# A third pair of nodes in plain float32 in the last stage, the flag's loads tied to an output, and two node splits emitted earlier

## The chip, the cores and the metric

The kernel runs on one core of a Trainium2 chip. The metric is the device time of one execution in microseconds (us). Before the change three runs took 454.33, 454.55 and 456.33 us; their median is 454.55 us.

## What is computed

The reference is a small graph network on 2,500 nodes with 256 features and 80,000 edges sorted by their end node. Cut to what matters:

```python
h = max(layernorm(x), 0)
xs = [h]
for W, b in ((W0, b0), (W1, b1), (W2, b2)):      # three edge convolutions
    m = concat([h[dst], h[src] - h[dst]]) @ W + b
    h = relu(segment_sum(m, dst) / max(count, 1))
    xs.append(h)
return x + concat(xs) @ Wf + bf
```

## The kernel before, in words

The edge sums are done as matrix products. From the edge lists the kernel builds a matrix of edge counts (it lies in DRAM as `a_dram`, in bf16, in five groups of up to 512 columns), and a convolution is then a product of the counts with the node features, plus a product with the node's own features. That is `by_windows`. If some edge found no place in that scheme, a flag `missing` is set and `general` computes everything again behind a branch (`gnn_kernel`); for these inputs the flag stays 0.

**Layout.** 2,500 nodes are 20 tiles of 128, the last one not full, or Q = 10 pairs of tiles, q = 0 to 9; pair q holds tiles 2q and 2q + 1. `hT` holds the features of the present layer, transposed. `acc` holds the result, 20 tiles of 128 x 256, to which each layer's share of the last product is added (`add_to_acc`, on VectorE). At the end `acc` is written out.

**Products in three parts.** TensorE multiplies float32 quickly only in a reduced form (`fp32r`). So a float32 operand is first *split* (`Split`, line 1005): one ScalarE instruction makes the high part, two VectorE instructions (`rest`) make a low part and a mixed part. `times` (line 1234) then takes three products per chunk, twelve for a pair of tiles with 256 output columns. A pair in `PLAIN` (line 1484) is not split in the last stage: its product is taken from `hT` in plain float32, four matmuls in the program (lines 1571 to 1574), which stand in the profile as eight. Split parts lie in the pool `stage` (four buffers, tiles named `staged`, also used for the loads of counts) or, by `split_in_blocks` (line 1065), in the pool of `block` tiles.

**Order of the work.** Instructions of PE, DVE, ACT, POOL and SP that are issued through the wrapper `InOrder` (`PEo`, `DVEo` and so on) keep the order in which the program text emits them on their engine: an edge without a wait ties each to the one before. Anything else may be moved by the scheduler to where it takes the instruction's inputs to be ready. So the order in the text decides.

**Layers 1 and 2** (loop at line 1492). A *node stage* goes over the ten pairs in the order `orders[l]`. Step i multiplies pair `order[i]` (`Nodes.multiply`, which needs that pair's split), then `parts` takes the result from the banks (ScalarE scales it to `zf` and casts it to `zh`, VectorE makes `zl` and adds to `acc`; the last tile's `zf` is made on VectorE with `brow`), `combine` and `sums` make further forms, and `lone.multiply(i - 2)` does a part of the count product. At the end of step i the split of pair `order[i + 2]` is emitted (at i = 0 that of `order[3]`). A *stream stage* (`Stream`) then does the rest of the count products; its `tick` also emits the first splits of the next stage.

**The last stage** (line 1566) multiplies each pair of `orders[3]` by the last block of `Wf`: pair 8, 9, 0, 1 (split in the stream stage before), 2 (plain), 3 (split in blocks), 7 (plain), 6 (begun in the stream stage, its rest at i = 0), 5, 4. For each pair: products on PE, two `add_to_acc` on DVE, and the outputs. Up to i = 5 a pair (pair 9 excepted) goes out as one DMA of SP; from i = 6 on each tile goes alone, the first of a pair on SP's queue and the second on ACT's. Behind the adds of i = 1, 2, 3 stand the splits of pairs 3, 5 and 4.

**The flag** (line 1602). Each engine loads the flag into a register and branches on it (line 1607). SP's and POOL's loads run as soon as the flag is known. Those of PE, DVE and ACT are tied behind everything emitted on their engine. After the branch SP waits for the outputs, and all engines meet at the end of the program (line 1631).

Of the kernel before, what the change touches and what calls it, by code (L numbers as in the profile page):

```python
# [298 lines left out]
def by_windows(ctx: ExitStack, tc: tile.TileContext, x, src, dst, Ws, bs, Wf, bf, out, missing):  # L299
# [37 lines left out]
    Q = NT // 2  # L337
# [41 lines left out]
    def bank():  # L379
        return ps[-1].tile([P, 512], F32, name="bank")  # L380
# [75 lines left out]
    def load_wb(l, queue=SP):  # L456
        if l:
            new_raw(l)
        ws[l] = wpool.tile([P, DC, D], F32, name="wt"), raws[l][:, :, 0, :] if l else hot.tile([P, DC, D], F32, name="own_w0", bufs=1)
        queue.dma_start(ws[l][1], Ws[l][D:2 * D, :].rearrange("(c p) d -> p c d", p=P))  # L460

    def load_wt(l, queue=SP):
        queue.dma_start(ws[l][0], Ws[l][0:D, :].rearrange("(c p) d -> p c d", p=P))

    def load_wf(l, queue=SP):
        if l == L:
            new_raw(l)
        wfs[l] = raws[l][:, :, 1, :] if l else hot.tile([P, DC, D], F32, name="own_w1", bufs=1)
        queue.dma_start(wfs[l], Wf[l * D:(l + 1) * D, :].rearrange("(c p) d -> p c d", p=P))
# [24 lines left out]
    def load_b(l, queue=SP):  # L494
        queue.dma_start(brow[PAD:PAD + 1, :], bs[l].rearrange("(o d) -> o d", o=1))
# [39 lines left out]
    behind = pp.tile([P, WG * P], BF16, name="behind")  # L535
# [29 lines left out]
    ahead = []  # L565
# [258 lines left out]
    def group_of(g):  # L824
        return g * GS, min(GS, N - g * GS)
# [97 lines left out]
    order = """  # L923
# [73 lines left out]
    splits, coming = {}, []  # L997

    def block():
        return blocks[0].tile([P, 2, 512], F32R, name="block")  # L1000

    def flat(l):
        return raws[l].rearrange("p c t d -> p c (t d)") if l < L else wfs[l]
# [61 lines left out]
    def split_in_blocks(q, whole=True):  # L1065
        two = [block().rearrange("p c n -> p (c n)") for _ in range(2)]
        return Split(q, [two[0][:, :2 * D], two[0][:, 2 * D:], two[1][:, :2 * D]], whole)
# [356 lines left out]
    def all_found():  # L1424
        pf = bank()
        PEo.matmul(pf[0:1, 0:1], found, ones, start=True, stop=True)
        DVEo.tensor_scalar(missing, pf[0:1, 0:1], float(E), None, op0=OP.not_equal)
# [3 lines left out]
    def load_alone(k, order):  # L1431
        c = order[2 * k] // 2
        st = stage.tile([P, 8 * GS], BF16, name="staged").rearrange("p (t n) -> p t n", n=GS)[:, :4, :group_of(alone)[1]]
        SPo.dma_start(st, a_dram[alone][:, 4 * c:4 * c + 4, :group_of(alone)[1]])
        loaded[k] = st
# [45 lines left out]
                tick(n)  # L1481

    AHEAD_H = 2
    PLAIN = (2, 7)
    LAG = 2
    orders = [None, list(range(Q)), [8, 9, 0, 1, 2, 3, 7, 6, 5, 4], [8, 9, 0, 1, 2, 3, 7, 6, 5, 4]]
    def split(q):
        tile_ = stage.tile([P, 4 * GS], F32R, name="staged")
        Split(q, [tile_[:, k * 2 * D:(k + 1) * 2 * D] for k in range(3)])

    begun, bias = [], add_bf()
    for l in range(1, L):
        order = orders[l]
        lone = Alone(l, order)
        if l == 1:
            load_alone(0, order)
            split(order[2])
        pending = []
        stream = Stream(l)
        for i in range(Q + LAG):  # L1500
            if 0 < i <= Q:
                lone.make(i - 1)
            if i < Q:
                q = order[i]
                n = Nodes(l, q)
                n.multiply(splits.pop(q), coming[0])
                if i + AHEAD_H < Q and i % 2 == 1:
                    load_alone((i + 1) // 2, order)
                n.parts()
                n.combine()  # L1510
                ahead = i + AHEAD_H + (i == 0)
                if ahead < Q and order[ahead] not in splits:
                    split(order[ahead])
                pending.append(n)
            if i and pending:
                pending.pop(0).sums()
            if i == 1:
                for o in range(DC):
                    lone.own(o, 0)
                if l == 1:  # L1520
                    all_found()
            if i >= LAG:
                lone.multiply(i - LAG)
            if i == Q - 1:
                stream.load(3)
        room = stage.tile([P, 4 * GS], F32R, name="staged")
        stream.make(2)
        lone.end()
        turn_of[1] = 0
        if l + 1 < L:  # L1530
            load_b(l + 1, SPo)
            load_wb(l + 1, SPo)
            load_wt(l + 1, SPo)
        load_wf(l + 1, SPo)
        after = orders[l + 1]

        def tick(n):
            if (l, n) in AT["bias"]:
                next(bias)
            if n == AT["begun"] and l + 1 == L:  # L1540
                begun.append(split_in_blocks(6, False))
            if n == AT["wsum"]:
                combine(wsum, ws[l][0].rearrange("p c (o n) -> p (c o) n", o=2))
                own_forms.append(Forms(ws[l][0], [ws[l][0][:, c, :] for c in range(DC)],
                                       [room[:, k * DC * D:(k + 1) * DC * D].rearrange("p (c d) -> p c d", c=DC)
                                        for k in range(3)]))
            for k, step in enumerate(("high", "low", "across", "last")):
                if n == AT["forms"][k]:
                    getattr(own_forms[-1], step)()
            if n == AT["sub"] and l + 1 < L:  # L1550
                DVEo.tensor_sub(ws[l + 1][0], ws[l + 1][0], ws[l + 1][1])
            if n == AT["load"] and l + 1 < L:
                load_alone(0, after)
            for k in range(3 if l + 1 < L else 4):
                if n == AT["split"][k]:
                    split(after[k])
            for k, step in enumerate(("high", "low", "across", "last")):
                if n == AT["coming"][k]:
                    if k == 0:
                        raw = flat(l + 1)  # L1560
                        coming[:] = [Forms(raw, [raw[:, c, :] if l + 1 < L else raws[L][:, c, 0, :] for c in range(DC)])]
                    getattr(coming[0], step)()

        stream.run(tick)

    order = orders[L]
    for i, q in enumerate(order):
        po = bank()
        po = [po[:, :D], bank()[:, :D] if i == Q - 1 else po[:, D:]]
        for k in range(2):  # L1570
            if q in PLAIN:
                for c in range(DC):
                    PEo.matmul(po[k], hT[:, c, (2 * q + k) * P:(2 * q + k + 1) * P], wfs[L][:, c, :],
                               start=(c == 0), stop=(c == DC - 1))
            else:
                times(po[k], splits[q], k, coming[0])
        for k in range(2):
            t = 2 * q + k
            add_to_acc(t, po[k])
            n = P if t < NT - 1 else LAST  # L1580
            if i < Q - 4 and q < Q - 1:
                if k:
                    d = SPo.dma_start(out[(t - 1) * P:(t + 1) * P, :].rearrange("(k p) d -> p k d", p=P),
                                      acc[:, t - 1:t + 1, :])
            else:
                d = (ACTo if i >= Q - 4 and k else SPo).dma_start(out[t * P:t * P + n, :], acc[:n, t, :])
        if i == 0:
            begun[0].rest()
        elif i == 1:
            split_in_blocks(3)  # L1590
        elif i < 4:
            split((5, 4)[i - 2])


def gnn_kernel(tc: tile.TileContext, x, src, dst, Ws, bs, Wf, bf, out):
    nc = tc.nc
    with tc.tile_pool(name="flag", bufs=1) as flag:
        missing = flag.tile([1, 1], I32, name="missing")
        tc.mark_branch_hint_location("again", "LikelyTaken",
                                     engines=[getattr(mybir.EngineType, e) for e in ("PE", "DVE", "Activation")])  # L1600
        by_windows(tc, x, src, dst, Ws, bs, Wf, bf, out, missing)
        loads, (again,) = nc.values_load_multi_w_load_instructions(missing, min_val=0, max_val=1)

        for d in loads:
            if d.ins.engine in [getattr(mybir.EngineType, e) for e in ("PE", "DVE", "Activation")]:
                tc.keep_in_program_order(d)
        with tc.If(again > 0, label="again"):
            general(tc, x, src, dst, Ws, bs, Wf, bf, out)

# [27 lines left out]
```

## Time and profile before

| what | value |
|---|---|
| runs of before, us | 454.33, 454.55, 456.33 |
| the profiled execution's own time, us | 454.44 |
| its span, first to last instruction, us | 452.5 |
| mean granted clock of TensorE | 0.995 |
| ScalarE (ACT) busy, us | 326.2 (72%) |
| GpSimd (POOL) busy, us | 53.7 (12%) |
| HBM read, written | 35.23 MB, 18.14 MB |
| last stage's outputs | 1 x 68 KB, 5 x 128 KB and 5 x 256 KB on SP's queue, 4 x 128 KB on ACT's |

The profile comes from one execution. Its span leaves out what lies around the first and the last instruction, 1.94 us here. In a timeline row the first number is the start from the span's begin, the second how long the merged group took, then engine, line, operation, the tiles written and read, and the number of instructions; in brackets the idle time of the engine before it and what ended it. Nearly all instructions carry line 267, that of the `InOrder` wrapper, so they are told apart by their tiles: `bank<-block,staged` are products of split pairs, `bank<-wbf,hT` those of plain ones, `staged<-hT` the high part of a split (on ACT) or `staged<-hT,staged` its low part (on DVE). PEld is TensorE's weight load; one goes ahead of each matmul. A row of a table by stretches holds the stretch, its length, then busy time and number of instructions of the engines in the order PE, PEld, DVE, ACT, POOL (or of the one asked for), the granted clock, the mean busy share of the 16 DMA engines and GB/s.

### The profile page before, as it was taken

To read this page: it belongs to the slowest core of one execution; us is meant where nothing else is said; L and a number is where in the kernel's file an instruction comes from. 1 tells how busy PE (TensorE), PEld (TensorE's weight loads), DVE (VectorE), ACT (ScalarE), POOL (GpSimd) and SP (SyncE) were. 2 spreads that over 40 slices of the span, in tenths; PEclk is the share of its full clock that TensorE was granted. 3 is DMA by queue.
4 is the path that set the end of the run, shared out by engine and by line. 5 is a ranking of instruction groups with operands and counts; after the bars stand their busy time and mean duration, and the time that the engine had idled before them with its cause. 6 is when DMAs were issued, how large, how long until landed. Compare 5 with 4: busy or idle time off the path is not lost.

```text
span 452.5 us, 7520 instructions
## 1 busy us (share of the span) xinstructions
PE 441.5 (98%) x2755; PEld 360.1 (80%) x2755; DVE 379.4 (84%) x735; ACT 326.2 (72%) x610; POOL 53.7 (12%) x68
## 2 busy tenths in 40 slices
PE   7999999999999999999999999999999999999993
PEld 3888877888888889888878878867788788788793
DVE  7999999998899536399968958997999789589894
ACT  5898888777765427577789949875887898597630
POOL 4791201302006030100000000000000000000000
PEclk9999999999999999999999999999999999999998
DMA  8410199792959997611483432211135525241015
GB/s 275 118 39 1 24 198 165 88 170 35 202 117 109 183 245 124 136 43 44 167 314 92 151 131 95 93 42 41 42 83 183 211 94 185 94 124 62 1 65 167
DMA packets 34377, 53.77 MB, mean 119 GB/s; under 512 B 1963, under 2 KB 27774, under 8 KB 34334
## 3 DMA queue, kind: packets, MB, share of 16 engines
q0 software_dynamic: 14624, 19.00, 26.3%
q1 hardware_dynamic: 18206, 32.59, 22.3%
q10 hardware_dynamic: 1504, 1.63, 1.1%
q8 instruction: 23, 0.38, 0.3%
q14 instruction: 20, 0.16, 0.1%
HBM read 35.23 MB, written 18.14 MB: 118 GB/s over the span
## 4 chain that ended last, share of the span: by engine, by line


## 5 line engine op out<-in xcount | busy, mean ns | idle before, releaser
L267 ACT CAST block<-staged 128x1024 fp32r<-128x1024 bf16 (+1 forms) x120 | 116.8, 1026 | 1.7 <-DVE staged L267 1.6
L267 PE MATMUL bank<-a,zh 128*128 128x512 f32 (+1 forms) x200 | 79.5, 397 | 0.0
L267 PE MATMUL bank<-a,zl 128*128 128x512 f32 (+1 forms) x200 | 77.1, 385 | 0.0
L267 PE MATMUL bank<-block,zh 128*128 128x512 f32 (+1 forms) x200 | 76.7, 384 | 0.0
L267 PE MATMUL bank<-block,zl 128*128 128x512 f32 (+1 forms) x200 | 76.0, 380 | 0.0
L267 ACT CAST a<-bank 128x480 fp32r<-128x480 f32 (+2 forms) x107 | 53.1, 561 | 25.7 <-PE bank L267 25.6
L267 DVE TENSOR_TENSOR one_m<-iota_m,key_m 128x2048 bf16<-128x2048 bf16 (+3 forms) x55 | 64.3, 1170 | 5.2 <-PE bank L267 5.2
L267 PE MATMUL bank<-block,sh 128*128 128x512 f32 x160 | 64.3, 402 | 0.0
L267 PE MATMUL bank<-block,staged 128*128 128x512 f32 (+1 forms) x288 | 62.4, 367 | 0.2 <-DVE staged L267 0.2
L267 PE MATMUL bank<-block,sl 128*128 128x512 f32 x160 | 62.4, 390 | 0.0
L267 PEld LDWEIGHTS bank<-block,staged 128*128 128x128 f32 x288 | 49.2, 189 | 9.8 <-DVE staged L267 1.0
L267 DVE TENSOR_TENSOR block<-staged 128x1024 fp32r<-128x1024 bf16 x40 | 47.2, 1220 | 0.9
L267 PEld LDWEIGHTS bank<-a,zh 128*128 128x128 f32 x200 | 37.6, 188 | 7.0 <-issue 0.5
L267 PEld LDWEIGHTS bank<-a,zl 128*128 128x128 f32 x200 | 37.6, 188 | 6.9 <-issue 0.5
L267 DVE TENSOR_TENSOR one_n<-iota_n,key_n 128x640 bf16<-128x640 bf16 (+3 forms) x110 | 43.0, 432 | 0.0
L267 PEld LDWEIGHTS bank<-block,zl 128*128 128x128 f32 x200 | 37.5, 188 | 6.7 <-issue 0.4
L267 PEld LDWEIGHTS bank<-block,zh 128*128 128x128 f32 x200 | 37.5, 188 | 6.7 <-issue 0.4
L267 PEld LDWEIGHTS bank<-block,sh 128*128 128x128 f32 x160 | 30.0, 188 | 8.6 <-ACT block L267 1.7
L267 PEld LDWEIGHTS bank<-block,sl 128*128 128x128 f32 x160 | 30.1, 188 | 6.8 <-issue 1.0
L267 PEld LDWEIGHTS <-one_m 128*128 128x128 bf16 x840 | 29.3, 97 | 7.6 <-issue 4.2
L267 PE MATMUL bank<-own_w,hT 128*128 128x256 f32 x144 | 34.8, 384 | 0.0
L267 POOL DMA_DIRECT2D a_dram<-a x24 | 21.1, 1098 | 101.9 <-ACT a L267 93.7
(197 smaller groups left out, 676.9 us busy)
## 6 DMA issues: line engine op xcount, KB each, us to landing
staged<-a_dram SPq DMA_DIRECT2D x40, 512.0 KB
a_dram<-a POOLq DMA_DIRECT2D x20, 640.0 KB, 10.2
staged<-a_dram SPq DMA_DIRECT2D x10, 452.0 KB
a_dram<-a POOLq DMA_DIRECT2D x4, 565.0 KB, 12.3
acc<-in_x_dram POOLq DMA_DIRECT2D x3, 640.0 KB, 21.1
out_dram<-acc SPq DMA_DIRECT2D x5, 256.0 KB
acc<-in_x_dram SPq DMA_DIRECT2D x2, 512.0 KB
acc<-in_x_dram ACTq DMA_DIRECT2D x1, 768.0 KB
```

The source lines that it names most:

```text
L267: return self.tc.keep_in_program_order(call(*args, **kwargs))
```

## The change

Three edits:

- **Plain pairs.** `PLAIN` gets pair 3, and the last stage's order has 2, 7, 3, 6 in place of 2, 3, 7, 6. The split of pair 3 in blocks is gone; the splits of pairs 5 and 4 stand behind the adds of i = 1 and i = 2.
- **The flag's loads.** `by_windows` returns the last DMA of step i = Q - 2 = 8 (ACT's output of tile 11, the second tile of pair 5). The loads of PE, DVE and ACT are no longer tied to the order of their engine; they get a dependency, with a wait, on that DMA.
- **Node splits.** In the node stages of layers 1 and 2 the splits emitted at steps i = 0 and i = 2 stand ahead of that step's `parts` and `combine` instead of behind them. In layer 2 these are the splits of pairs 1 and 2, in layer 1 of pairs 3 and 4.

```diff
-    PLAIN = (2, 7)
+    PLAIN = (2, 7, 3)
...
-    orders = [None, list(range(Q)), [8, 9, 0, 1, 2, 3, 7, 6, 5, 4], [8, 9, 0, 1, 2, 3, 7, 6, 5, 4]]
+    orders = [None, list(range(Q)), [8, 9, 0, 1, 2, 3, 7, 6, 5, 4], [8, 9, 0, 1, 2, 7, 3, 6, 5, 4]]
...
+                ahead = i + AHEAD_H + (i == 0)
+                new = ahead < Q and order[ahead] not in splits
+                if new and i in (0, 2):
+                    split(order[ahead])
                 n.parts()
                 n.combine()
-                ahead = i + AHEAD_H + (i == 0)
-                if ahead < Q and order[ahead] not in splits:
+                if new and i not in (0, 2):
                     split(order[ahead])
...
+            if i == Q - 2:
+                near_end = d
         if i == 0:
             begun[0].rest()
-        elif i == 1:
-            split_in_blocks(3)
-        elif i < 4:
-            split((5, 4)[i - 2])
+        elif i < 3:
+            split((5, 4)[i - 1])
+    return near_end
...
-        by_windows(tc, x, src, dst, Ws, bs, Wf, bf, out, missing)
+        near_end = by_windows(tc, x, src, dst, Ws, bs, Wf, bf, out, missing)
...
         for d in loads:
             if d.ins.engine in [getattr(mybir.EngineType, e) for e in ("PE", "DVE", "Activation")]:
-                tc.keep_in_program_order(d)
+                tc.add_manual_dep(d.ins, near_end.ins.name,
+                                  mybir.DependencyInfo(mybir.DependencyClass.Sync, mybir.DependencyReason.DATA),
+                                  reason="behind the outputs")
```

## The prediction, made before the result was known

> **What bounds the kernel now.** I read first the busy times, then the stretch after the last matmul, then the engines' queues back from there. All times are microseconds from the span's start.
>
> The page's first part:
>
> ```profile
> PE 441.5 (98%) x2755; PEld 360.1 (80%) x2755; DVE 379.4 (84%) x735; ACT 326.2 (72%) x610; POOL 53.7 (12%) x68
> ```
>
> TensorE is busy nearly always, so what PE loses before its last matmul is lost for the kernel. Behind that matmul another chain decides. The last stretch of VectorE's and PE's timelines:
>
> ```profile
> 435.17 0.87 DVE L267 SCALAR_TENSOR_TENSOR acc<-bank,share,acc 128x256 f32<-128x256 f32 x2
> ...
> 440.18 0.68 DVE L267 TENSOR_TENSOR staged<-hT,staged 128x512 fp32r<-128x512 f32 x1
> 440.90 0.69 DVE L267 SCALAR_TENSOR_TENSOR staged<-staged 128x512 fp32r<-128x512 f32 x1
> 441.51 4.78 DVE L267 SCALAR_TENSOR_TENSOR acc<-bank,share,acc 128x256 f32<-128x256 f32 x12
> ```
>
> ```profile
> 442.41 3.04 PE L267 MATMUL bank<-block,staged 128*128 128x256 f32 x24
> ```
>
> PE ends at 445.45, the last `add_to_acc` at 446.29. The twelve adds of the last six pairs have no gap, 0.39 apart, so DVE is behind PE here. It still owed a split (440.18 to 441.51, 1.33) when PE had long finished pair 2. All six pairs' outputs, 1.5 MB, therefore leave after 442.3. Table by stretches (engines' busy times, then clock, DMA share, GB/s):
>
> ```profile
> 444.20:448.60 4.40, 1.25 (x11) 1.04 (x9) 2.09 (x6) 0.00 (x0) 0.00 (x0) 0.94 0.92 297
> 448.60:449.00 0.40, 0.00 (x0) 0.00 (x0) 0.00 (x0) 0.00 (x0) 0.00 (x0) 0.50 0.23 87
> 449.00:450.00 1.00, 0.00 (x0) 0.00 (x0) 0.00 (x0) 0.00 (x0) 0.00 (x0) 0.50 0.07 24
> 450.00:452.50 2.50, 0.00 (x0) 0.00 (x0) 0.00 (x0) 0.00 (x0) 0.00 (x0) 0.50 0.00 0
> ```
>
> The 16 DMA engines are full until 448.6. Then one alone works on: 0.07 of 16 is one engine. It ends at 450.0, and 2.5 more pass to the span's end. So the end is set by the slowest DMA engine's last output. Why one engine is late, the queue rows for 446.5 to 448.6 and for 448.6 to 450.1 show:
>
> ```profile
> q8 instruction: 1, 0.02, 2.6%
> ```
>
> ```profile
> q14 instruction: 3, 0.02, 3.9%
> ```
>
> One instruction fetch took 0.026 x 16 x 2.1 = 0.87, three more 0.039 x 16 x 1.5 = 0.94 together, in the midst of the outputs. That they shared the late engine is my inference: 1.8 of fetches against 1.4 of lateness. They follow the branches behind the flag's loads (duration, then the start):
>
> ```profile
> L1602 PEldq TENSOR_LOAD <-missing x1: 771/771/771, 443.1 to 443.1; - x1
> L1602 DVEq TENSOR_LOAD <-missing x1: 1134/1134/1134, 445.5 to 445.5; - x1
> L1602 ACTq TENSOR_LOAD <-missing x1: 767/767/767, 446.7 to 446.7; - x1
> ```
>
> ```profile
> L1607 SPq EVENT_SEMAPHORE  x8: 17/17/17, 447.6 to 450.8; - x8
> ...
> L1607 PEldq COMPARE_BRANCH  x1: 1212/1212/1212, 444.0 to 444.0; - x1
> ...
> L1607 DVEq COMPARE_BRANCH  x1: 84/84/84, 446.7 to 446.7; - x1
> L1607 ACTq COMPARE_BRANCH  x1: 68/68/68, 447.5 to 447.5; - x1
> ```
>
> ```profile
> L1631 SPq DRAIN x3: 7/7/7, 451.6 to 451.9; - x3
> ...
> L1631 ACTq DRAIN x2: 8/8/8, 448.1 to 451.9; - x2
> ```
>
> SP's eight waits are for the outputs. SP reaches its drain at 451.6, ACT at 448.1: the flag's own chain has 3.5 to spare today.
>
> **Part 1, two splits sooner.** PE's one loss in layer 2's node stage (weight loads):
>
> ```profile
> 323.43 0.19 PEld L267 LDWEIGHTS bank<-block,staged 128*128 128x128 f32 x1
> 324.05 0.19 PEld L267 LDWEIGHTS bank<-block,staged 128*128 128x128 f32 x1 [0.44 <-DVE staged L267]
> 324.78 2.14 PEld L267 LDWEIGHTS bank<-block,staged 128*128 128x128 f32 x10 [0.54 <-DVE staged L267]
> ...
> 328.62 2.70 PEld L267 LDWEIGHTS bank<-block,staged 128*128 128x128 f32 x12
> ```
>
> Twelve loads take 2.70 where nothing is waited for; these took 324.78 + 2.14 - 323.43 = 3.49. The loss is 0.79. They wait for the split emitted at step i = 2, whose two DVE instructions stand at 323.31 and 324.03:
>
> ```profile
> 313.03 0.69 DVE L267 TENSOR_TENSOR zl<-tmp,zh 128x512 fp32r<-128x512 f32 x1 [2.85 <-ACT zh L267]
> ...
> 315.41 0.68 DVE L267 TENSOR_TENSOR staged<-hT,staged 128x512 fp32r<-128x512 f32 x1
> ...
> 316.74 0.48 DVE L267 SCALAR_TENSOR_TENSOR tmp<-bank,share,brow 128x256 f32<-128x256 f32 x1
> ...
> 323.31 0.69 DVE L267 TENSOR_TENSOR staged<-hT,staged 128x512 fp32r<-128x512 f32 x1
> 324.03 0.69 DVE L267 SCALAR_TENSOR_TENSOR staged<-staged 128x512 fp32r<-128x512 f32 x1
> ...
> 328.34 0.69 DVE L267 SCALAR_TENSOR_TENSOR staged<-staged 128x512 fp32r<-128x512 f32 x1
> ```
>
> ```profile
> 309.61 2.01 ACT L267 ACTIVATE hT<-hT 128x1024 f32<-128x1024 f32 x2 [2.63 <-DVE hT L267]
> ...
> 312.37 0.62 ACT L267 CAST zh<-tmp 128x512 fp32r<-128x512 f32 x1
> 312.90 0.63 ACT L267 ACTIVATE staged<-hT 128x512 fp32r<-128x512 f32 x1
> ```
>
> A split is one ACT and two DVE instructions and no DMA, so SP and POOL are not touched. The second move alone only permutes DVE's row, which has no gap from 318 on: the split ends 2.4 sooner and PE's wait goes, but PE, 0.79 earlier, then needs the next split's last part at 328.3, and that still ends at 329.03. The gain would be given back. The first move pays for it. Its ACT half runs right after the Relus (311.5), its DVE half into the 2.85 idle. On ACT it pushes zh by 0.53 (312.37 to 312.90, as one such instruction takes), so DVE's zl starts at 313.56; but the 1.33 from 315.41 to 316.74 is gone, and the `brow` step, for which ACT's next zh waits, comes at 316.74 + 0.53 - 1.33 = 315.94. DVE runs 0.80 earlier from there, the next split ends at 328.23, and the gain stands with 0.06 to spare. I take -0.79; bounds -0.04 (given back) and -0.82. In layer 1 no PE weight load of the stage waits for a split, so the same moves cost nothing while ACT's waits for PE's banks cover the 0.53 in front of the first copies; uncovered it would cost up to 0.53.
>
> **Part 2, a third plain pair.** Weight loads by pair (the four split pairs 8, 9, 0, 1; plain pair 2; split pair 3):
>
> ```profile
> 430.30:435.97 5.67, 5.63 (x48) 1.00 0.14 48
> 435.97:437.60 1.63, 1.45 (x9) 1.00 0.35 102
> 437.60:439.13 1.53, 1.50 (x13) 1.00 0.08 27
> ```
>
> A split pair behind a split pair takes 5.67 / 4 = 1.42, behind a plain one 1.53; a plain one 1.63 behind a split one. Plain behind plain isn't in the trace: between 1.63 and, if the 0.10 that a change of kind costs falls on it as well, 1.73; I take 1.72. Pairs 2, 3, 7, 6 took 1.63 + 1.53 + 1.63 + 1.53 = 6.32; 2, 7, 3, 6 will take 1.63 + 1.72 + 1.72 + 1.53 = 6.60. PE loses 0.28 (bounds 0.10 to 0.30). The Trainium skill, "FP8 and Floating Point Precision", section "TensorE Precision Notes", counts four passes for true float32; against the three products of a split pair that would be an estimated 1.9 per plain pair and +0.5 here. The trace has 1.63, so it costs less here than that.
>
> PE ends at 445.45 - 0.79 + 0.28 = 444.94. DVE loses a split (1.33), ACT one instruction that nobody waited for. The adds of pairs 2, 7, 3 and 6 then run from 441.51 - 1.33 - 0.80 = 439.4; those of 5 and 4 wait for PE, no longer for DVE. The last add ends at about 444.94 + 0.05 + 0.47 = 445.46 (before 446.29).
>
> **Part 3, the outputs.** What a tile takes when nothing is in its way, a single output early in the stage (same table):
>
> ```profile
> 436.45:437.05 0.60, 0.60 (x5) 0.52 (x4) 0.57 (x2) 0.00 (x0) 0.00 (x0) 1.00 0.72 231
> ```
>
> Its add (435.17, the first of two) ended at 435.64 and its bytes at 437.05: 1.4. At the end of before the tiles lie in a queue instead: the last add ends at 446.29, its bytes at 448.6 on an undisturbed DMA engine and at 450.0 on the late one. After, pair 2 leaves at 440.2 instead of 442.3. Twelve tiles of 131 KB at the 0.297 MB/us of the first row above are 0.44 each, 5.3; first bytes come 0.8 behind an add (435.64 to 436.45), so the queue itself would be done by 440.2 + 0.8 + 5.3 = 446.3. The last tile's own way ends later, at 445.46 + 1.4 = 446.9. An early fetch remains:
>
> ```profile
> q8 instruction: 1, 0.02, 1.0%
> ```
>
> (441 to 446.5: 0.010 x 16 x 5.5 = 0.9, and PE's sequencer still comes to that place.) Put whole on one engine it gives 446.3 + 0.9 = 447.2 there at worst; I take 447.0.
>
> **Part 4, the flag's loads.** They now wait until ACT's output of i = 8 (tile 11, pair 5) has landed. Behind each load stand only its engine's branch and drain, and at the far end SP's barrier. That output's add ends 1.44 before the last one (two tiles of pair 4 at 0.72), 444.0; bytes by 445.4, or 446.0 on the late engine; SP's last wait, at 450.8, came 0.8 behind the last byte, so the loads start by 446.2 to 446.8. ACT needs 448.1 - 446.7 = 1.4 from load to drain: 447.6 to 448.2. SP's drain stood 1.6 behind the last byte (450.0 to 451.6), after: 448.6. So the wait is hidden, by 0.4 to 1.0; each us by which the landing is later than that lengthens the kernel. PE's fetch started 1.3 or more behind its branch (445.24 to 446.5 or later), so the fetches come at 447.9 or later, when the outputs are through: the 1.4 between 448.6 and 450.0 goes. If they still fell among them, it would cost the same 0.9 to 1.4 as today.
>
> **Sum.** Last byte 447.0 instead of 450.0; 2.5 behind it as now: span 449.5, -3.0 (0.8 from the earlier last add, 0.8 from the shorter queue, 1.4 from the fetches). The profiled execution took 454.44, 0.11 under the median of the three runs, 454.55. 454.44 - 3.0 = 451.4. Its own range is 450.8 (plain pairs at +0.10, bytes by 446.5) to 452.2 (fetch on the late engine in part).
>
> **Rivals.**
> A, the flag becomes the end. Now the branch stands behind a DMA's landing, and if the code behind it must first be fetched, all of PE, DVE and ACT wait for that at the very end. Load from 446.5, branch at 447.4, a fetch 1.3 until its start and 0.9 long: 449.6, drain 449.9, and 0.9 from SP's drain (451.6) to the end: span 450.8, 452.7 in all. For it: fetches do follow the branches here. Against: ACT's branch took 0.07 and its drain came 0.6 behind it (447.5, 448.1), before the three late fetches, so its code was there. The Trainium skill, "Runtime: NRT & Kernel Launch", section "Instruction fetch mechanics", says a taken branch beyond the current two pages has to fetch before it can go on; DVE and ACT show no such wait, and PE's 1.21 ends as its last weight load does. Chance 0.16.
> B, the queue stays. Outputs that leave sooner spread no better, fetches fall among them, and the last byte comes as far behind the last add as now. Only the 0.83 of the add is left: 453.6. Against: from 436.0 to 439.1 the DMA engines have room (share 0.35 and 0.08 in the table by pairs). Chance 0.13.
> C, part 1 is given back, since the split at 328.23 has but 0.06 to spare: everything 0.75 later, 452.2. Chance 0.10.
> D, slower. The loads are no longer pinned behind their engine's last instruction; if PE's is put ahead of pair 4's products, PE stands from 443.2 until the landing (446.5 at the middle). Load to 447.3, products 1.44 and the last one's 0.28, add 0.52: 449.5; output 1.4, end 2.5: span 453.4, 455.3. It decides from the point at which the load stands in PE's queue before pair 4; from 3.1 of standstill on the gain is used up. Against: in order of readiness pair 4 comes first, its split being done by 439.4. Chance 0.06.
> That the change doesn't do what it says (loads still early, so that the fetches hit the outputs): -1.6 to -2.1, 452.3 to 452.8. Chance 0.05.
>
> **How the numbers follow.** A measurement of this kernel can tell about 0.5%, 2.3 us, from no change: faster means below 452.3, slower above 456.8. The forecast, 451.4, has 0.50 and lies below 452.3 nearly whole (0.48); A gives 0.05 of its 0.16, since its fetch may be shorter; C 0.06, the last case 0.03: faster 0.62. B whole, the rest of A, C and the others: same 0.33. D's upper half, with a later landing, and what I don't see: slower 0.05. The range reaches down to 450.7 and up to 453.7, which takes in B; D and the far ends are left out.
>
> **What would show it.** Right: no wait for "DVE staged" in the weight loads of layer 2's node stage; three plain pairs in a row with some 5.1 of weight loads; gaps between the last four adds, each ended by PE; a last add near 445.5; DMA share below 0.9 from 441 to 446 and nothing moved behind 447.2; the instruction fetches behind the last output; SP's last wait near 447.8. Wrong: loads of the flag that end later than SP's last wait (A); an output byte behind 448 (B); a new "DVE staged" wait one pair later (C); a PE gap before its last twelve products (D).

## The result, and the profile after

Eight runs of the changed kernel have a median of 452.80 us (451.28 to 454.09); eight of the kernel before 455.45 (454.33 to 456.33). The ratio is 0.9939, 95% interval 0.9923 to 0.9954: 2.65 us faster, with an interval clear of 1, and inside the predicted range (451.4; 450.7 to 453.7). The profiled execution took 451.28 us, its span is 449.4, against 454.44 and 452.5 before.

The profile of each kernel is of one execution. Two profiles can be compared closely only from a common point, since the first part varies: the first product of layer 1's node stage starts at 192.8 to 194.0 in the fourteen profiles of this study. Its row in the timeline of PE, after (before: 192.86):

```profile
192.81 0.50 PE L267 MATMUL bank<-block,staged 128*128 128x512 f32 x1
```

From there to the end of the span it is 259.6 before and 256.6 after. All distances "from the first node product" below are counted from this instruction; between profiles only these are compared. The ratios and medians come from all runs.

**Layer 2's node stage.** The waits of PE's weight loads from 305 to 352 us, before and after (total, times, longest):

```profile
PEld bank L267 <- DVE staged L267: 1.0, 2, 0.5
```

```profile
PEld bank L267 <- DVE staged L267: 0.2, 1, 0.2
```

The two waits of 0.44 and 0.54 for a split are gone; one of 0.19 has come at 313.6, ahead of another product (`bank<-hT,wt`). To the first plain weight load of the last stage it is now 242.34 from the first node product, where it was 243.11: 0.77 less.

**The last stage.** Weight loads, then VectorE's adds, after:

```profile
435.15 5.06 PEld L267 LDWEIGHTS bank<-wbf,hT 128*128 128x128 f32 x24
440.23 1.60 PEld L267 LDWEIGHTS bank<-block 128*128 128x128 f32 x12
```

```profile
438.58 3.22 DVE L267 SCALAR_TENSOR_TENSOR acc<-bank,share,acc 128x256 f32<-128x256 f32 x8
442.08 0.88 DVE L267 SCALAR_TENSOR_TENSOR acc<-bank,share,acc 128x256 f32<-128x256 f32 x2 [0.28 <-PE bank L267]
443.52 1.27 DVE L267 SCALAR_TENSOR_TENSOR acc<-bank,share,acc 128x256 f32<-128x256 f32 x3 [0.56 <-PE bank L267]
444.96 0.48 DVE L267 SCALAR_TENSOR_TENSOR acc<-bank,share,acc 128x256 f32<-128x256 f32 x1 [0.17 <-PE bank L267]
```

Three plain pairs stand in a row, 24 loads in 5.06. The twelve adds without a gap have become eight, and the last three groups each wait for PE: the order of the two engines has turned round. The last add ends at 445.44 (before 446.29).

**The outputs.** Stretches after (engines' busy times, clock, DMA share, GB/s), then the code fetches: from 441 to 446, from 446 to 448.6, and from 448.6 to 449.4:

```profile
441.00:446.00 5.00, 3.92 (x33) 3.71 (x31) 3.43 (x9) 0.00 (x0) 0.00 (x0) 1.00 0.91 295
446.00:447.20 1.20, 0.00 (x0) 0.00 (x0) 0.00 (x0) 0.00 (x0) 0.00 (x0) 1.00 0.47 153
447.20:448.60 1.40, 0.00 (x0) 0.00 (x0) 0.00 (x0) 0.00 (x0) 0.00 (x0) 0.84 0.00 0
```

```profile
q8 instruction: 1, 0.02, 1.1%
```

```profile
q14 instruction: 1, 0.01, 1.4%
```

```profile
q8 instruction: 1, 0.02, 7.3%
q14 instruction: 2, 0.02, 5.1%
```

Nothing moves from 447.2 to 448.6: the outputs are through by 447.2 (before 450.0). Two fetches still fell among them: the 16 KB one near 443 that the kernel before has too (row on q8), and a small one (0.014 x 16 x 2.6 = 0.58). The other three come behind them.

**The flag and the end.** Loads, branches and drains after (duration, then the start):

```profile
L1606 ACTq TENSOR_LOAD <-missing x1: 471/471/471, 446.9 to 446.9; - x1
L1606 DVEq TENSOR_LOAD <-missing x1: 543/543/543, 446.9 to 446.9; - x1
L1606 PEldq TENSOR_LOAD <-missing x1: 489/489/489, 447.0 to 447.0; - x1
```

```profile
L1613 SPq EVENT_SEMAPHORE  x8: 17/17/17, 446.3 to 447.7; - x8
...
L1613 PEldq COMPARE_BRANCH  x1: 492/492/492, 447.6 to 447.6; - x1
```

```profile
L1637 SPq DRAIN  x3: 7/7/7, 448.5 to 448.8; - x3
L1637 ACTq DRAIN  x2: 8/8/8, 448.0 to 448.8; - x2
L1637 PEldq DRAIN  x2: 8/8/8, 448.3 to 448.9; - x2
L1637 DVEq DRAIN  x2: 10/14/17, 448.3 to 448.9; - x2
```

SP's last wait for an output begins at 447.7 (before 450.8), its drain at 448.5 (451.6). PE and VectorE reach theirs at 448.3. The flag's chain, which had 3.5 us to spare, has about 0.2 now.

### The profile page after: what moved, and what is told of

The parts are those of the page before. It is cut to its first block, busy times and chain, and to the rows that moved or that the text cites. A ratio compares the mean times of both kernels' runs of the same rounds, so it can differ in the third digit from the quotient of the medians.

```text
span 449.4 us, 7513 instructions
## 1 busy us (share of the span) xinstructions
PE 441.4 (98%) x2751; PEld 360.3 (80%) x2751; DVE 378.4 (84%) x733; ACT 326.0 (73%) x609; POOL 53.9 (12%) x68
## 3 DMA queue, kind: packets, MB, share of 16 engines
q10 hardware_dynamic: 1504, 1.63, 1.1%
## 4 chain that ended last, share of the span: by engine, by line
PE 92%; DVE 3%; POOL 3%; DMA 1%; issue 1%; ACTq 0%
PE bank L267 92%; DVE st L267 1%; POOL acc L267 1%; DMA dst_i<-in_dst_dram 1%; POOL es L267 1%; POOL ed L267 1%; DVE mv L267 0%; DVE acc L267 0%; DVE pick L267 0%; DVE behind L267 0%; DVE end_f L267 0%; DVE start_i L267 0%; DVE off L267 0%; DVE rs L267 0%; DVE first L267 0%
```

## The experiments

The theory after the result: the gain has three roots, PE's lost wait (0.8), a shorter queue of outputs, and code fetches that come behind the outputs; the flag's chain is hidden, but barely. The main rival: the flag's chain is or can become the end (rival A of the prediction), and the second move of a split is needed, or not. "Changed kernel" means the kernel with all three edits. This table is from the traces and runs; distances are from the first node product, "branch" is PE's branch behind the flag, "PE program" the number of instructions in PE's program up to and with that branch, counted in the built program, "fetch" the start of the last 16 KB fetch on q8 that begins ahead of 446 us (none: it comes later).

| kernel | ratio to before, 95% interval | to first plain load | to last add's end | to span's end | PE program | fetch | branch |
|---|---|---|---|---|---|---|---|
| before | 1 | 243.11 | 253.44 | 259.62 | 3628 | 442.8 | 1.21 |
| changed kernel | 0.9939, 0.9923 to 0.9954 | 242.34 | 252.63 | 256.61 | 3624 | 443.0 | 0.49 |
| e1 splits alone | 0.9973, 0.9956 to 0.9990 | 242.29 | 252.62 | 258.66 | 3630 | 442.4 | 1.19 |
| e2 plain pair alone | 0.9977, 0.9961 to 0.9994 | 243.20 | 253.49 | 257.99 | 3621 | none | 3.71 |
| e3 flag alone | 0.9975, 0.9958 to 0.9992 | 243.09 | 253.41 | 258.34 | 3629 | 443.3 | 0.49 |
| e4 flag pinned | 0.9960, 0.9943 to 0.9977 | 242.30 | 252.59 | 257.56 | 3623 | 443.8 | 1.93 |
| e5 second split only | 0.9993, 0.9976 to 1.0009 | 242.91 | 253.20 | 259.76 | 3622 | none | 3.87 |
| e6 first split only | 0.9951, 0.9932 to 0.9970 | 242.40 | 252.69 | 256.76 | 3624 | 443.3 | 0.49 |
| e7 flag behind the last output | 0.9957, 0.9941 to 0.9973 | 242.30 | 252.60 | 257.13 | 3624 | 443.7 | 0.49 |
| e8 four units made | 0.9939, 0.9918 to 0.9961 | 242.39 | 252.68 | 256.78 | 3624 | 444.2 | 0.49 |
| e9 = e5, PE program + 2 | 0.9965, 0.9953 to 0.9977 | 242.94 | 253.23 | 257.50 | 3624 | 444.1 | 0.49 |
| e10 = changed, PE program - 2 | 0.9965, 0.9946 to 0.9985 | 242.38 | 252.67 | 259.38 | 3622 | none | 4.02 |
| e11 = e2, PE program + 2 | 0.9978, 0.9964 to 0.9992 | 243.04 | 253.33 | 258.42 | 3623 | 444.2 | 1.89 |
| e12 = changed, PE program + 2 | 0.9941, 0.9924 to 0.9959 | 242.32 | 252.61 | 256.70 | 3626 | 443.4 | 0.49 |

### The three edits alone

**e1_splits_alone**: the kernel before with the two node splits sooner, and nothing else.

```diff
+                ahead = i + AHEAD_H + (i == 0)
+                new = ahead < Q and order[ahead] not in splits
+                if new and i in (0, 2):
+                    split(order[ahead])
                 n.parts()
                 n.combine()
-                ahead = i + AHEAD_H + (i == 0)
-                if ahead < Q and order[ahead] not in splits:
+                if new and i not in (0, 2):
                     split(order[ahead])
```

> Before with the two node splits moved and nothing else. My theory: PE's wait for the split in layer 2's node stage (0.79 us) goes, the first move pays for it in VectorE's row, and the end stays as it was behind the last add (add at 446.3 of a span of 452.5). So the last add comes 0.8 earlier and the span is 451.7, ratio 0.998. Rival (given back): the wait comes back at the next pair, span 452.4, ratio 1.000, and the weight loads show a new wait for DVE staged.

Measured: 454.36 us, 0.9973. The last stage begins 0.82 earlier, the last add ends 0.82 earlier, the span 0.96. The wait in layer 2 is gone as in the changed kernel, and the tail behind the last add stays at 6.0 (before 6.2). So this part keeps its whole 0.8 and gives nothing to the tail.

**e2_plain_alone**: the kernel before with the third plain pair and its order.

```diff
-    PLAIN = (2, 7)
+    PLAIN = (2, 7, 3)
...
+    orders = [None, list(range(Q)), [8, 9, 0, 1, 2, 3, 7, 6, 5, 4], [8, 9, 0, 1, 2, 7, 3, 6, 5, 4]]
...
-        elif i == 1:
-            split_in_blocks(3)
-        elif i < 4:
-            split((5, 4)[i - 2])
+        elif i < 3:
+            split((5, 4)[i - 1])
```

> Before with the third plain pair and one split less, nothing else. My theory: PE ends 0.28 later (445.73), the last add no later than before (446.25), the outputs spread over more time, so that the undisturbed DMA engines end near 447.7 instead of 448.6; the flag's fetches still fall among the outputs and one engine ends at 448.5 to 449.0. Span 451.0 to 451.5, ratio 0.997. Rival (the queue is as long as before, the end hangs on the last add alone): span 452.4, ratio 1.000.

Measured: 454.86, 0.9977. PE ends 0.38 later, the last add 0.05 later than before, and yet the span ends 1.63 earlier: the tail shrinks from 6.2 to 4.5. Most of that is a shorter queue. Stretches of this kernel:

```profile
446.00:447.40 1.40, 0.58 (x5) 0.38 (x4) 0.93 (x3) 0.00 (x0) 0.00 (x0) 1.00 0.61 198
447.40:448.00 0.60, 0.00 (x0) 0.00 (x0) 0.00 (x0) 0.00 (x0) 0.00 (x0) 1.00 0.64 208
```

The DMA engines are no longer full from 446 to 448, where in the kernel before they were (0.92 from 444.2 to 448.6). But one of the two 16 KB fetches that fell among the outputs of the kernel before is also gone from there. In e11, below, which has the same edit, both are back, and the tail is 5.1: by these profiles 1.1 of the 1.7 is the queue's, and up to 0.6 belongs to that fetch. PE's branch took 3.71 here, which nobody expected; see below.

**e3_flag_alone**: the kernel before with the flag's loads behind step 8's output.

```diff
+            if i == Q - 2:
+                near_end = d
...
-                tc.keep_in_program_order(d)
+                tc.add_manual_dep(d.ins, near_end.ins.name,
+                                  mybir.DependencyInfo(mybir.DependencyClass.Sync, mybir.DependencyReason.DATA),
+                                  reason="behind the outputs")
```

> Before with the flag's loads behind the output of tile 11 and nothing else. My theory: the three late instruction fetches and PE's no longer fall among the outputs, the last byte moves from 450.0 to 448.6, span 451.1, ratio 0.997; the loads start near 448.3, close to the end. Rival 1 (the flag's chain becomes the end): the engines' drains come behind SP's, span 452 or more. Rival 2 (the fetches were not what held the one DMA engine): an engine still ends 1.4 behind the others, span 452.5, ratio 1.000.

Measured: 454.10, 0.9975. The last add stands where it was (253.41), and the tail falls from 6.2 to 4.9. The stretches of this kernel at its end:

```profile
446.00:449.20 3.20, 0.02 (x1) 0.00 (x0) 0.86 (x3) 0.00 (x0) 0.00 (x0) 0.81 1.02 334
449.20:449.60 0.40, 0.00 (x0) 0.00 (x0) 0.00 (x0) 0.00 (x0) 0.00 (x0) 0.50 0.06 23
```

All engines are full to 449.2 and then done together; the DMA engine that worked alone for 1.4 in the kernel before is no longer there. So the late engine goes when the fetches come behind the outputs, and that is worth 1.3.

**e4_flag_pinned**: the changed kernel with the loads tied to their engine's order again, as before.

```diff
-                tc.add_manual_dep(d.ins, near_end.ins.name,
-                                  mybir.DependencyInfo(mybir.DependencyClass.Sync, mybir.DependencyReason.DATA),
-                                  reason="behind the outputs")
+                tc.keep_in_program_order(d)
```

> After with the flag's loads pinned in their engines' order again (the other two edits kept). My theory: the fetches come back among the outputs, PE's from about 446.3, the other three near 447.5; the last byte moves from 447.2 to 447.9 to 448.5; span 450.2 to 450.8 against 449.4 of after, ratio to before 0.996. Rival (with outputs this early the fetches miss them): span 449.4 or less, the same as after.

Measured: 453.61, 0.9960. The adds end as in the changed kernel (252.59), the span 0.95 later. From 446 to 449 the fetches are back among the outputs, 0.029 + 0.024 of 16 engines for 3 us, 2.5 in all:

```profile
q10 hardware_dynamic: 296, 0.27, 28.0%
q1 hardware_dynamic: 205, 0.18, 17.8%
q14 instruction: 3, 0.02, 2.9%
q8 instruction: 1, 0.02, 2.4%
```

So the third edit is worth 1.0 on top of the others and 1.3 alone. The three alone give 0.96, 1.63 and 1.28, 3.87 together; all at once they give 3.01. Half of the difference goes when e11, with 1.20, stands for the plain pair in place of e2: 3.44. That the other half is shared, because a shorter queue leaves the fetches less to disturb, is an argument and not shown.

### Which split pays

**e5_second_split_only** and **e6_first_split_only**: the changed kernel with one of the two moves undone.

```diff
-                if new and i in (0, 2):
+                if new and i == 2:
                     split(order[ahead])
                 n.parts()
                 n.combine()
-                if new and i not in (0, 2):
+                if new and i != 2:
```

(e6 has 0 in the place of 2.)

> The changed kernel with the split of step i = 0 back behind its step; only that of i = 2 is sooner. Theory: VectorE's queue in layer 2's node stage is then 0.8 longer at that place, PE's wait moves to the next pair's split and the gain of part 1 is given back: one PEld wait for DVE staged of 0.5 to 1.0 us in the stage, 0.5 to 0.8 us slower than the changed kernel, ratio to before 0.9955 to 0.997. Rival: the second move is enough, no wait over 0.3 us, the time of the changed kernel (ratio 0.994 to 0.995).

> The changed kernel with only the split of step i = 0 sooner; that of i = 2 stands behind its step again. Theory: VectorE is 0.8 earlier from i = 0 on, the split of i = 2 ends near 323.9 in place of 324.7, and PE's 0.8 us wait shrinks to 0.1 or nothing: the time of the changed kernel within 0.2 us (ratio 0.994 to 0.995), the first move is the one that pays. Rival: both moves are needed; a wait for DVE staged of 0.5 us or more is left and the time is 0.5 to 0.8 us above the changed kernel's.

Weight loads of e5 in layer 2's node stage:

```profile
328.62 0.19 PEld L267 LDWEIGHTS bank<-block,staged 128*128 128x128 f32 x1
329.13 0.19 PEld L267 LDWEIGHTS bank<-block,staged 128*128 128x128 f32 x1 [0.33 <-DVE staged L267]
329.86 2.11 PEld L267 LDWEIGHTS bank<-block,staged 128*128 128x128 f32 x10 [0.54 <-DVE staged L267]
```

With the second move alone the wait has gone from the pair at 323 to the next one, as the theory said: the last stage begins 0.57 later than in the changed kernel, and only 0.20 of the 0.8 is left. With the first move alone no such wait is left, and the last stage begins within 0.06 of the changed kernel's. The first move does the work; the second is worth 0.06. The rival that both are needed falls.

But e5 came out at 455.3, no gain at all, 2.5 over the changed kernel where 0.5 to 0.8 was expected. The span says where: the tail behind the last add is 6.6 instead of 4.0.

### The branch that waits for its code

In e5 PE's branch takes 3.87:

```profile
L1613 SPq EVENT_SEMAPHORE  x8: 17/17/17, 447.1 to 449.2; - x8
...
L1613 PEldq COMPARE_BRANCH  x1: 3867/3867/3867, 448.4 to 448.4; - x1
```

SP has nothing more to wait for at 449.2; PE drains at 452.5, and all meet behind it. This is rival A. The moved split is no work of PE's: its products are the same, 2751 as in the changed kernel. But where PE waits for something has changed, and with it the number of instructions in PE's program, 3622 against 3624 ahead of the branch. In e5 and e2, the two with a long branch and the shortest programs, a fetch is missing that all the others make on q8 near 443. So the theory: it is a matter of where the branch lies in PE's code. To test it, the program was made two instructions longer or shorter by one idle warm-up product at the kernel's start, where PE waits for data anyway.

**e9_second_split_pe_plus2** (e5), **e11_plain_pe_plus2** (e2), **e12_after_pe_plus2** (the changed kernel), each with one product more, and **e10_after_pe_minus2** (the changed kernel) with one fewer:

```diff
-    WARM = {"next": 7, "pk00": 3, "T0": 3, "Z0": 2}
+    WARM = {"next": 8, "pk00": 3, "T0": 3, "Z0": 2}
```

(e10 has 6.)

> The kernel with the second split alone moved (whose PE branch behind the flag took 3.87 us) with one more idle warm-up product at the kernel's start: PE's program is two instructions longer ahead of the branch, 3624 as in the changed kernel in place of 3622, and nothing else differs. Theory (place of the code): whether PE's next 16 KB of code are fetched near 443 or only behind the flag's load hangs on how many PE instructions stand ahead of the branch; with 3624 the fetch comes near 443 to 444, the branch takes 0.5 us, and the span from the first node product falls by 2.3 to 2.6 us, to 0.6 above the changed kernel's; ratio to before 0.994 to 0.997. Rival (order on DVE and ACT, or chance): the branch stays at 3.5 to 4 us and the ratio at 0.998 to 1.000.

> The changed kernel with one idle warm-up product fewer at the kernel's start: PE's program is two instructions shorter ahead of the branch (3622 in place of 3624). Theory (place of the code): no fetch near 443, the PE branch takes 3.5 to 4 us in place of 0.49, all engines meet behind it, the time is 2.3 to 3.0 us above the changed kernel's and its whole gain is gone: ratio to before 0.998 to 1.001. Rival: the branch stays at 0.5 us and the ratio at 0.993 to 0.995.

> The plain pairs alone with one idle warm-up product more at the start (3623 PE instructions ahead of the branch in place of 3621). Theory: the 16 KB fetch comes near 443 to 444 again, PE's branch takes 1.2 to 1.9 us in place of 3.7 us; since it was not the last to end there (PE drain 0.8 ahead of SP's last wait), the time moves by less than 0.8 us; ratio to before 0.996 to 0.999. Rival: the late fetches set that kernel's end as well, and it falls by over 1 us, ratio below 0.996.

> Control: the changed kernel with one idle warm-up product more at the start (3626 PE instructions ahead of the branch in place of 3624). Theory: the branch stays near 0.5 us, the added product of 0.4 us lies in front of a wait of 0.3 us and costs 0 to 0.2 us; ratio to before 0.993 to 0.995. Rival: the idle product itself moves the time by more than 0.5 us, and then the two runs above say nothing on code.

The branch and SP's waits of e10, its queues from 441 to 448.7 and its fetches from 448.7 to 450.5, and its drains:

```profile
L1613 SPq EVENT_SEMAPHORE  x8: 17/17/17, 446.5 to 448.8; - x8
...
L1613 PEldq COMPARE_BRANCH  x1: 4022/4022/4022, 447.8 to 447.8; - x1
```

```profile
q1 hardware_dynamic: 1392, 1.31, 51.8%
q10 hardware_dynamic: 576, 0.52, 20.7%
q14 instruction: 1, 0.01, 0.5%
```

```profile
q8 instruction: 1, 0.02, 5.7%
q14 instruction: 2, 0.02, 2.3%
```

```profile
L1637 SPq DRAIN  x3: 7/7/7, 452.1 to 452.4; - x3
...
L1637 PEldq DRAIN  x2: 8/8/8, 452.1 to 452.5; - x2
```

One idle product fewer at 1.6 us, and the branch at 447.8 takes 4.02 instead of 0.49: no q8 fetch up to 448.7, then one of 0.057 x 16 x 1.8 = 1.64, and the span ends 2.77 later than in the changed kernel. In e9 one product more takes the branch from 3.87 to 0.49 (its row below) and the span's end forward by 2.26, to 0.89 behind the changed kernel's, of which 0.60 is e5's split.

```profile
L1613 PEldq COMPARE_BRANCH  x1: 487/487/487, 448.5 to 448.5; - x1
```

The control e12 is the changed kernel again (256.70 against 256.61; 452.90 us). So the place of the code is what sets PE's branch. In all fourteen kernels the line runs between 3622 and 3623 instructions; the changed kernel stands at 3624. In the seven where the branch took over 0.5, early fetch or late, it ended 1.4 to 1.6 behind the end of that fetch: in the kernel before the fetch ends at 443.69 and the branch at 445.23, in e10 at 450.39 and 451.84.

Over all runs the price is smaller: by medians e5 to e9 is 1.7 us (1.3 by the ratios to before; the two ran on different chips) and e12 to e10 1.1, with intervals that touch or overlap. The ratio of e10, 0.9965, misses the 0.998 to 1.001 that was expected and lies between that and the rival's 0.993 to 0.995. Whether the late code falls in every execution of e5 and e10 isn't shown.

e11 shows the other side: there too the fetch near 444 is back and the branch falls from 3.71 to 1.89, but the time stays (0.9978 against 0.9977). In e2 the load wasn't tied to an output, so the branch began at 445.2 and ended 1 us ahead of SP's last wait. So the late code costs where the branch stands behind the landing, and in e2 it cost nothing.

### How thin the cover is

**e7_flag_behind_last**: the changed kernel with the loads behind the very last output.

```diff
-            if i == Q - 2:
+            if i == Q - 1:
```

> The changed kernel with the flag's loads behind the very last output (i = Q - 1) in place of i = Q - 2. Theory: the changed kernel has only about 0.25 us between PE's, VectorE's and ScalarE's drains (448.3) and SP's (448.5); the last output is seen 0.8 to 1.0 us later, the loads begin near 447.8, the drains come near 449.2, and the span grows by 0.6 to 0.8 us (ratio to before 0.995 to 0.997). Rival: the barrier hides it, and the time stays that of the changed kernel; or a fetch of code falls into the exposed chain and it is 1.5 us or more above it.

Measured: 453.62, 0.9957. SP's last wait comes where it did (254.92 against 254.91 from the first node product), yet the span ends 0.52 later (0.6 to 0.8 was expected). The drains of e7:

```profile
L1637 SPq DRAIN  x3: 7/7/7, 449.9 to 450.2; - x3
...
L1637 PEldq DRAIN  x2: 8/8/8, 449.8 to 450.3; - x2
L1637 DVEq DRAIN  x2: 10/14/17, 449.8 to 450.2; - x2
```

SP's drain now follows PE's and VectorE's by 0.1 where it followed its own waits before. The flag's chain is the end, and one output earlier it was hidden by just enough.

### A version that might be faster

**e8_four_made**: the changed kernel, with more of the stream stage's counts cast ahead, against PE's waits for `block` at its start.

```diff
-        stream.make(2)
+        stream.make(4)
         lone.end()
```

> The changed kernel with four units of the stream stage's counts made ahead of the lone products' end in place of two. At the start of each stream stage PE's weight loads wait three times for ACT's block (0.6 to 0.7 us in a layer, two such layers). Theory: those waits go and the time falls by 0.5 to 1.3 us below the changed kernel (ratio to before 0.991 to 0.993). Rival: the makes come before work that PE needs sooner (the lone products' last parts on ACT), or buffers are not free, and the time is the same or up to 1 us longer.

Measured: 452.51 us, but the changed kernel's ratio to its own before, 0.9939 (0.991 to 0.993 was expected), and 242.39 to the last stage against 242.34. The waits of PE's weight loads from 230 to 240, changed kernel and e8:

```profile
PEld bank L267 <- ACT block L267: 0.7, 3, 0.3
```

```profile
PEld bank L267 <- ACT block L267: 0.4, 1, 0.4
```

The wait shrank, the time did not: measured by the lag behind the changed kernel, PE gains 0.26 at the first of those loads (234.8) and has lost all of it again by 236.7, two chunks of counts later, in the one wait of 0.4 for ScalarE's `block`. Why ScalarE isn't further ahead by then isn't settled. No faster version was found.

## Why the prediction was right, point by point

**Part 1**: -0.79 was forecast, and the splits alone gave 0.82. That the second move alone is given back was right, and e5 shows the wait one pair later, at the place named. What was missed is that the first move makes the second superfluous: an 0.8 earlier DVE lets the split of i = 2 end early enough by itself. Rival C was right as a mechanism and not the case.

**Part 2**: +0.28 on PE was forecast; from the first plain load to PE's end it took 9.48 before (445.45 - 435.97) and takes 9.77 after, +0.29. Three plain pairs took 5.06 of weight loads, some 5.1 forecast. So plain behind plain costs the dearer 1.72, not 1.63. Of the Trainium skill's four passes ("FP8 and Floating Point Precision", section "TensorE Precision Notes") an estimate of +0.5 came out; the trace has 0.29. The last add was forecast at 445.46 and ended at 445.44. The adds of pair 6 waited for PE as well as those of 5 and 4 (0.28).

**Part 3**: last byte 447.0 forecast, by 447.2 measured. The extra came with a fetch on q14 that was not in the sum. The sign "DMA share below 0.9 from 441 to 446" was a wrong one: the share is 0.91, up from 0.61 before, since the outputs begin earlier and the queue lies just there. The plain pair shows the shorter queue by itself (tail 6.2 to 4.5 in e2, to 5.1 in e11), so rival B falls.

**Part 4**: the fetches behind the outputs were right, in time (448.7; at 447.9 or later was forecast) and in worth: 1.4 forecast, 1.28 alone (e3), 0.95 on top of the rest (e4). SP's drain came at 448.5 (448.6). Two things were off. The loads began at 446.9, not by 446.8. And the cover was taken from ScalarE's drain, "by 0.4 to 1.0"; PE and VectorE drain 0.3 behind ScalarE, and the cover is 0.2. e7 shows that it is no more.

**The rivals.** A, at 0.16, was nearer than its argument: ScalarE's quick branch said nothing of PE's code, and two instructions fewer in PE's program would have brought the stall. Nothing in the prediction chose the 3624, so that A stayed away was luck. The sign was there and was read wrongly: PE's 1.21 was put down to its last weight load, which ended at the same time in the kernel before, but in e4 and e11 the branch ends 0.7 behind the last weight load (446.25 to 445.53, 446.67 to 446.00). In all three it ends 1.5 behind the end of the fetch, so the 1.21 is better read as a wait for code already. The price of A was too low too. The branch was put at 2.2 (1.3 to the start of the fetch, 0.9 long); in e10 it took 0.9 to the start, 1.6 for the fetch and 1.5 more from there to its end, 4.02. On "Runtime: NRT & Kernel Launch", section "Instruction fetch mechanics", the Trainium skill's rule that a taken branch whose target isn't at hand waits for a fetch agrees with these 4.02 us, and the 0.49 of the changed kernel shows the case without it. D did not occur: the last twelve products have no gap.

**The sum**: 449.5 forecast for the span, 449.4 measured; -3.0 forecast, -3.01 from the first node product. The medians moved by 2.65. That the profiled execution, 451.28, meets the forecast of 451.4 so closely is in part luck: it was the fastest of the eight, and their median, 452.80, is 1.4 above it.

## What to carry to other kernels

When the end of a kernel is a queue of outputs, look for what else uses those DMA engines at that moment, code fetches included, and for the instruction that sets them off; tying it behind an output that lands shortly before the end moves them out of the way as long as what stands behind it stays hidden. Before trusting a small difference between two variants, compare the tail behind the last work apart from the work, and PE's branch in both: a variant can lose 1 to 2 us (e10, e5) to the place of its code and nothing to its idea. Of two edits that are made together, undo each by itself; here one of two splits did all.

## What the runs showed of the hardware

- Two instructions more or fewer in PE's program, put at its start, decide whether its branch at the end takes 0.49 or 3.9 to 4.0 us (e5 to e9, the changed kernel to e10). A 16 KB fetch at 442 to 444 is there in the one case; in the other (e2, e5, e10) it begins 0.9 to 1.3 behind the branch's start. That PE's sequencer asks for it only when it has come to a certain place, behind the flag's load in the one case, fits all fourteen kernels, but no trace shows which instruction asks. All fourteen also carry a hint for this branch (`mark_branch_hint_location` in `gnn_kernel`); no run leaves it out, so its part is open.
- A late branch ended 1.4 to 1.6 us behind the end of its 16 KB fetch in all seven profiles that show one (before, e1, e2, e4, e5, e10, e11); where the fetch had ended 3.5 us or more before the branch began, the branch took 0.49.
- A fetch on q8 takes 0.9 us and up to 1.64 (e10), and one on q14 0.3 to 0.7. In the kernel before 1.8 us of them stood among the last outputs and one DMA engine ended 1.4 behind the others; with them behind the outputs (e3) none did.
- The stretch up to the first node product varied by 1.2 us between these profiles, about what a single edit here is worth. e8 was already 1.2 behind the changed kernel at 31.8 us, where PE's instructions are the same in both, and kept it to 234 us.
